# A decoder layer on one Trainium2 core: which PSUM bank side products may take in crowded slots, where dt's second part is placed, and a lock of its own for LayerNorm's tile

## The chip, the cores and the metric

The kernel runs on one NeuronCore of a Trainium2 chip. Its engines are TensorE (PE in the profile; PEld are its weight loads), VectorE (DVE), ScalarE (ACT), GpSimd (POOL) and SyncE (SP, which here only issues DMAs). Each engine works through its own instructions in the order in which the program lists them. The metric is the time of one execution on the device in microseconds; lower is better.

## What is computed

One pre-norm decoder layer on x of shape (16, 256, 512), in float32, with a context of the same shape:

```python
x = x + mamba2(layernorm(x))          # 32 heads of 64, state 64, convolution of 4 taps
x = x + xattn(layernorm(x), ctx, ctx) # sigmoid features, k times v summed over positions, then cumulative over heads
x = x + ffn(layernorm(x))             # ternary weights, 8 bit activations, gate and up 2048 wide
```

The attention part adds sigmoid(q wq + bq) times a state: sigmoid(k wk + bk) times the values, summed over the positions of a batch, and cumulative over the heads; the feed-forward part rounds its inputs to 8 bits and its weights to three values. The change lies in what surrounds the first part:

```python
def _mamba2(x, W_in, conv_w, conv_b, A_log, D_param, dt_bias, norm_w, W_out):
    xz = x @ W_in
    z, xBC, dt_proj = xz[..., :2048], xz[..., 2048:4224], xz[..., 4224:]
    xBC_c = silu(causal_conv_of_4_taps(xBC, conv_w) + conv_b)
    x_conv, B_ssm, C_ssm = xBC_c[..., :2048], xBC_c[..., 2048:2112], xBC_c[..., 2112:]
    dt = jax.nn.softplus(dt_proj + dt_bias)
    A = -jnp.exp(A_log)
    def step(h, inp_t):
        x_t, dt_t, B_t, C_t = inp_t
        dA = jnp.exp(A[None, :] * dt_t)
        h = dA[:, :, None, None] * h + dt_t[:, :, None, None] * x_t[..., None] * B_t[:, None, None, :]
        y_t = jnp.einsum('bhds,bs->bhd', h, C_t) + D_param[None, :, None] * x_t
        return (h, y_t)
    y = scan_over_positions(step) * silu(z)
    var = jnp.mean(jnp.square(y), axis=-1, keepdims=True)
    return (norm_w * (y * jax.lax.rsqrt(var + EPS))) @ W_out
```

## The kernel before

**Tiling.** The 16 batches are taken as 8 pairs k, the 2048 inner channels as 16 chunks c of 128. One step of the main loop is a slot s = 16 k + c: one chunk of one pair. The loop runs over s = 2 to 127, with its first two slots and a last part written out apart; then the feed-forward part goes over 32 tiles of 128 rows. In the profile the written-out start ends at about 45 us and the slots at about 1515 us.

**One slot's own work**, in TensorE's order: the projection to z (12 matmuls of 512 columns, L676), with turn_x (L941, four transposes of the last chunk's convolved x) put in after the sixth; the projection to x (12 more); scan_out of the last chunk (py, L961 and L968); the product with W_out for the chunk before that (po, L1011). VectorE: times_g, the product of the last chunk's decays with B and C's matrix (L929, L933); the chunk's two scans (L912); the three taps of the convolution (L693, writing xs); D x and the gate (L976, L981). ScalarE: silu of z (L891), the convolution's first tap (L897), silu of xs (L906), scalings (L920, L951) and others. GpSimd: the low halves of y (L988) and sums of squares (L999). So turn_x of a slot needs silu of the taps of the slot before, and scan_out needs times_g.

**The order is written by hand.** A slot has 8 points, now = 8 s + 0 to 7; at each, advance(now) lets side tasks (Python generators) issue their next step. A step says how many points to wait (wait), at which points of a slot it may be issued, on which engine and how many us it is taken to need; a planner's allowance (room, for VectorE 2.3 us in each half of a slot) holds it back when that engine has been given enough, unless the step is marked with leaves, which must go. Tasks are asked in the order of their rank. The side tasks are: LayerNorm of the next pair or of a batch's queries (norm_transposed), dt for the next pair (time_steps), B and C for the next pair (states), the context (context_pair, context_group), the rest of a batch's attention (batch_end) and the quantising of the feed-forward weights.

**dt** (time_steps) has these steps on VectorE: part 1 (L724 to L731), then exp on ScalarE (L733), part 2a (L735 to L739), part 2b (L742 to L745, a row of fourteen small operations with 2a), then exp, a transpose on TensorE and a short scan. **B and C** (states): a projection of 12 matmuls, the first tap on ScalarE (L791), three taps on VectorE (L693, writing bcT), then silu. **The residual** (mixed, four operations L1037 on VectorE, after L1028 and a power on GpSimd) is written out in the third slot of each pair from the third pair on (s = 34, 50, 66, ...), ahead of that slot's times_g.

**PSUM banks.** A side product needs a bank. Class Banks hands out two: "own", one tile kept for this, at point 7; and "z" at point 3, between the projection to x and scan_out, which is one tile of the ring ps_p with two buffers in which the slot's two projections stand:

```python
if self.free["z"] and others and others[0] is me:
    hold = "z"
```

With z taken, the next slot's first projection is the third tile after the x projection in a ring of two, so it waits until the taps have read that one.

**Locks.** Shared(n) is a counter of n that tasks take and give in the order of the program's making; it keeps a task from reusing a tile whose last user has not been issued. lns (1) guards LayerNorm's tiles: y ("ln", the normalised rows in float32), and its two float16 halves hi and lo, from which two transposing DMAs read. It was held from the load to the transposes. The small statistics tiles have two buffers.

**SP's queue** carries, in every slot, the loads of the decays (L837, L847) and of W_out's chunk (L538, two buffers: issued after L1011 of its slot, used two slots later), from some slots weights (L412), and the side tasks' transposes (L652), loads (L614, L1046, L1066, L1095) and stores (L1135, L1400).

Of the kernel before, what the change touches and what calls it, by code (L numbers as in the profile page):

```python
# [58 lines left out]
def decoder_kernel(  # L59
# [135 lines left out]
    with ExitStack() as part:  # L195
# [19 lines left out]
        WAIT = "wait"  # L215
# [3 lines left out]
        POINTS = 8  # L219
# [10 lines left out]
        def dve(us, wait=2):  # L230
            return (wait, (1, 2, 5, 6), "dve", us) if steady() else (soon(), range(POINTS), "dve", us)
# [30 lines left out]
        def leaves(step):  # L262

            return *step, True
# [3 lines left out]

        clock = [0]

        class Shared:
            def __init__(self, free):
                self.free = free
# [14 lines left out]
        class Banks:  # L288
# [8 lines left out]
            def take(self, own=False, first=False):  # L297
                me = [own]
                self.line.insert(0 if first else len(self.line), me)
                while True:  # L300
                    moment = clock[0] % POINTS
                    if steady() and moment == 3:

                        others = [one for one in self.line if not one[0]]
                        if self.free["z"] and others and others[0] is me:
                            hold = "z"
                            break
                    elif self.free["own"] and self.line[0] is me and (
                        not steady() or moment == 7 and clock[0] >= self.since
                    ):  # L310
                        hold = "own"
                        break
                    yield WAIT
                self.line = [one for one in self.line if one is not me]
                self.free[hold] = False
                return hold
# [8 lines left out]
        def misc(hold, shape, name):  # L325
# [2 lines left out]
            }[hold]  # L328
            return ps.tile(shape, F32, tag=tag, name=name)

        chunks, stages, lns, turned, turned_q, attends, ctxs, outs, xs, late, preps, streams = (
            Shared(n) for n in (3, 3, 1, 2, 1, 1, 1, 2, 3, 1, 2, 2)
        )


# [270 lines left out]
            yield  # L606
        def norm_transposed(src, b, what, store):

            yield from lns.take(rank=0 if what == "m" else 2 if "late" in store else 1)
            y = p1.tile([P, NT, D], F32, tag="ln", name=f"ln_{what}_{b}")  # L610
            if src is None:
                src = y
                yield moved(1.3, 1)
                nc.sync.dma_start(y, x[b].rearrange("(i p) d -> p i d", p=P))  # L614
                yield landed()
            mv = p2.tile([P, NT, 2], F32, tag="ln_mv", name=f"ln_mv_{what}_{b}")
            rs = p2.tile([P, NT], F32, tag="ln_rs", name=f"ln_rs_{what}_{b}")
            yield leaves(dve(1.7)) if what == "m" else dve(1.7)
            for i in range(NT):
                st = p2.tile([P, 6], F32, tag="ln_st", name=f"ln_st_{what}_{b}_{i}")  # L620
                nc.vector.bn_stats(st, src[:, i, :])
                nc.vector.bn_aggr(mv[:, i, :], st)
            nc.vector.tensor_scalar(rs, mv[:, :, 1], EPS, LN_UP**-2, ALU.add, ALU.mult)
            hi = p1.tile([P, NT, D], F16, tag="ln_hi", name=f"lnh_{what}_{b}")
            lo = p1.tile([P, NT, D], F16, tag="ln_lo", name=f"lnl_{what}_{b}")
            nc.vector.tensor_scalar(mv[:, :, 1], mv[:, :, 0], -1.0, None, ALU.mult)
            yield 1, range(POINTS), "pool", 1.5
            nc.gpsimd.tensor_tensor(rs, rs, mhalf[:, 0:NT], ALU.pow)
            nc.gpsimd.tensor_tensor(mv[:, :, 1], mv[:, :, 1], rs, ALU.mult)
            yield act(2.3, 2)  # L630
            for i in range(NT):
                nc.scalar.activation(
                    y[:, i, :], src[:, i, :], AF.Identity,
                    scale=rs[:, i : i + 1], bias=mv[:, i, 1:2],
                )
            nc.scalar.copy(hi, y)
            yield pool(2.4)
            nc.gpsimd.tensor_tensor(lo, y, hi, ALU.subtract)
            if what == "q":
                yield from turned_q.take(rank=2 if "late" in store else 1)  # L640
                store["q"] = [
                    p1.tile([P, NT, KD, P], F16, tag=f"lnT_{n}_q", name=f"lnT_{n}_q_{b}") for n in "hl"
                ]
                dst = store["q"]
            else:
                if b % 2 == 0:
                    yield from turned.take()
                    turned_tiles(store, b)
                dst = [t[:, b % 2] for t in store["lnT"]]
            for t, part_ in zip(dst, (hi, lo)):  # L650
                yield moved(1.2, 4 if part_ is hi else 1)
                nc.sync.dma_start_transpose(  # L652
                    t.rearrange("p i k t -> p (i k) t"), part_.rearrange("p i d -> p (i d)")
                )
            lns.give()
            if what == "q" or b % 2:
                yield landed(12 if what == "m" else 8)
                store["ready", what] = True
# [39 lines left out]
        def time_steps(pair):  # L698
# [3 lines left out]
            k = pair["k"]  # L702
            hold = yield from bank.take(first=True)
            pd = misc(hold, [P, NT, 2, NH], f"pd_{k}")
            for j in range(2):
                for i in range(NT):
                    n = 0
# [23 lines left out]
            nc.vector.scalar_tensor_tensor(v, r, -2.0, v, ALU.mult, ALU.add)  # L731
            yield alone()
            nc.scalar.activation(v, v, AF.Exp)  # L733
            yield dve(1.2)
            nc.vector.tensor_scalar(s, v, 2.0, None, ALU.add)  # L735
            nc.vector.reciprocal(s, s)
            nc.vector.tensor_tensor(s, s, v, ALU.mult)
# [39 lines left out]
        def states(pair):  # L777


            while ("ready", "m") not in pair:  # L780
                yield WAIT
            k = pair["k"]
            hold = yield from bank.take()
            raw = misc(hold, [P, 2, S], f"bc_{k}")
            project_pair(
                raw.rearrange("p b (i t) -> p (b i) t", i=NT), lambda wi, kc: w_bc16[:, wi, kc, :],
                pair,
            )
            yield leaves(act(0.8, 2))
            bcT = p1.tile([P, 2, S], F32, tag="bcT", name=f"bcT_{k}")  # L790
            nc.scalar.activation(  # L791
                bcT, raw, AF.Identity, scale=convw_bc[:, 3:4], bias=convb_bc
            )
            yield leaves(dve(2.3, 1))
            for j in (2, 1, 0):
                tap_of(bcT, raw, convw_bc, j)
            bank.give(hold)
            yield act(0.6)
            nc.scalar.activation(bcT, bcT, AF.Silu)
            yield issued()  # L800
            cT = p1.tile([NS, 2, S], F32, tag="cT", name=f"cT_{k}")
            if k:
                nc.sync.dma_start(cT, bcT[NS : 2 * NS])
            else:
                pc = misc("o3", [P, 2, S], "cT_first")
                nc.tensor.matmul(pc[0:NS], ident[:, NS : 2 * NS], bcT, start=True, stop=True)
                nc.scalar.copy(cT, pc[0:NS])
            yield landed()
            g = p2.tile([P, 2, 3, P], F32, tag="g", name=f"g_{k}")
            for j in range(2):  # L810
                yield pe(0.4)
                hold = yield from bank.take()
                pg = misc(hold, [P, 3, P], f"pg_{k}_{j}")
                for n, (s0, t0) in enumerate(((0, 0), (P, P), (0, P))):
                    nc.tensor.matmul(
                        pg[:, n, :], bcT[0:NS, j, s0 : s0 + P], cT[:, j, t0 : t0 + P],
                        start=True, stop=True,
                    )
                yield leaves(dve(0.7))
                nc.vector.tensor_tensor(  # L820
                    g[:, j, 0:2, :], pg[:, 0:2, :], upper.unsqueeze(1).to_broadcast([P, 2, P]),
                    ALU.mult,
                )
                nc.vector.tensor_copy(g[:, j, 2, :], pg[:, 2, :])
                bank.give(hold)
            pair["g"] = g
            yield
# [203 lines left out]
        def mixed(pair, ns=range(2 * NT)):  # L1031

            rq = pair["rq"]
            for n in ns:
                j, i = divmod(n, NT)
                xb = batches[2 * pair["k"] + j]["x"]
                nc.vector.scalar_tensor_tensor(  # L1037
                    xb[:, i, :], pair["po"][n], rq[:, n : n + 1], xb[:, i, :], ALU.mult, ALU.add
                )
# [463 lines left out]
        proj, m, tp, o2, o3 = (ps_p, "proj"), (ps_m, "m"), (ps_t, "tp"), (ps_o, "o2"), (ps_o, "o3")  # L1503
# [423 lines left out]
        for s in range(2, n_slots):  # L1927
# [5 lines left out]
            if u:  # L1933
                units[s + 2] = u
            if ended:
                mixed(ended)
                for j in range(2):
                    start(s, batch_end(batches[2 * ended["k"] + j]), rank=2)
# [147 lines left out]
```

## Time and profile before

| what | us |
|---|---|
| median of 3 runs (lowest, highest) | 1891.16 (1885.18, 1892.93) |
| the profiled execution's own time | 1887.74 |
| its span, first to last instruction | 1886.0 |
| PE busy in 0 to 45, 45 to 1515, 1515 to 1886 | 28.6, 1401.6, 351.7 |
| DVE busy in the same stretches | 33.1, 1275.7, 333.1 |
| ACT busy in the same stretches | 25.7, 969.0, 249.0 |
| POOL busy in the same stretches | 7.3, 625.2, 40.4 |

The mean granted clock of TensorE is 0.988 of full speed. The span is divided by the profile into 40 slices; in each, a digit is the busy share in tenths:

```profile
PE   6789999999999998999999999999999989999998
DVE  7899888777888889888988998989887879999997
```

TensorE is at nine tenths nearly everywhere, VectorE between seven and nine. A line of the table of groups has the line of the source, engine, operation, what is written and read, the count, and after the bar the busy time and the mean in ns:

```profile
L693 DVE SCALAR_TENSOR_TENSOR xs<-pp,convw_sb,xs 128x510 f32<-128x510 f32 (+2 forms) x384 | 286.3, 746 | 147.3 <-ACT xs L897 137.8
L912 DVE TENSOR_TENSOR_SCAN m<-dab,starts 128x512 f32<-128x512 f32 x254 | 302.4, 1232 | 0.0
```

The last part is the engine's idle time just before, with what ended most of it. A row of a table of waits is: engine and line that waited, "<-", what ended the wait, then us in total, how many times, and the longest. In a timeline the first column is the start in us, the second the duration, and a bracket at the end holds idle time before the instruction and what ended it.

### The profile page before, as it was taken

The numbers are of one execution on the slowest core, as the hardware profiler recorded it, in microseconds if no ns is written. First come the engines' busy times: TensorE is split into PE (matmuls) and PEld (weight loads), VectorE is DVE, ScalarE is ACT, GpSimd is POOL, SyncE is SP. The second block draws the span as 40 slices with busy tenths as digits, with TensorE's granted clock in tenths as the row PEclk, the third lists the DMA queues.
The fourth block names the chain that finished last, engine by engine and source line by source line (L and its number), as shares of the span: only waits on it lengthen the run. The fifth ranks groups of instructions, "written<-read, shape, count | busy, mean of one in ns | idle before, by whom it ended". The sixth has DMA issues, their size and how long they took to land.

```text
span 1886.0 us, 30370 instructions
## 1 busy us (share of the span) xinstructions
PE 1781.9 (94%) x10464; PEld 1016.7 (54%) x10464; DVE 1641.9 (87%) x2718; ACT 1243.6 (66%) x2889; POOL 673.0 (36%) x684
## 2 busy tenths in 40 slices
PE   6789999999999998999999999999999989999998
PEld 4355555555556555656555556555556544444443
DVE  7899888777888889888988998989887879999997
ACT  5677656676667665666666666666666647777675
POOL 1233433343334354546454536454532222100000
PEclk9899999999999999999999999999999999999999
DMA  5764775689669677877697779687777726555554
GB/s 168 235 185 147 234 197 176 210 261 233 171 180 296 185 196 232 264 177 183 209 251 211 202 198 266 192 190 184 246 198 200 250 70 123 133 115 122 107 118 98
DMA packets 296933, 358.95 MB, mean 190 GB/s; under 512 B 163765, under 2 KB 197861, under 8 KB 296778
## 3 DMA queue, kind: packets, MB, share of 16 engines
q1 hardware_dynamic: 277962, 296.13, 59.8%
q0 software_dynamic: 18240, 60.84, 9.4%
q8 instruction: 83, 1.36, 0.3%
q14 instruction: 72, 0.59, 0.1%
q10 hardware_dynamic: 576, 0.04, 0.0%
HBM read 279.70 MB, written 39.58 MB: 169 GB/s over the span
## 4 chain that ended last, share of the span: by engine, by line
PE 60%; DVE 25%; ACT 4%; DMA 4%; issue 4%; POOL 2%; SPq 0%; ACTq 0%; DVEq 0%; POOLq 0%
PE pp L676 22%; PE po L1011 12%; PE po_f L1621 5%; PE pu L1579 5%; PE pg L1579 5%; DVE m L912 4%; PE py L961 4%; DVE xs L693 4%; DVE m L929 2%; PE trx L941 2%; PE py L968 2%; DVE m L933 1%; DVE y L976 1%; DVE sp_q L742 1%; PE bc L676 1%
## 5 line engine op out<-in xcount | busy, mean ns | idle before, releaser
L676 PE MATMUL pp<-lnT_h_m,w 128*128 128x512 f16 (+1 forms) x2056 | 659.2, 382 | 21.9 <-DVE xs L693 21.1
L676 PEld LDWEIGHTS <-w 128*128 128x128 f16 x3084 | 295.9, 99 | 360.8 <-issue 34.3
L988 POOL TENSOR_TENSOR yl<-y,yh 128x512 fp32r<-128x512 f32 x128 | 179.9, 1406 | 712.5 <-ACT yh L987 627.2
L693 DVE SCALAR_TENSOR_TENSOR xs<-pp,convw_sb,xs 128x510 f32<-128x510 f32 (+2 forms) x384 | 286.3, 746 | 147.3 <-ACT xs L897 137.8
L676 PE MATMUL pp<-lnT_l_m,w 128*128 128x512 f16 (+1 forms) x1028 | 392.6, 382 | 0.0
L1011 PE MATMUL po<-wout,yh 128*128 128x512 f32 x1024 | 339.4, 413 | 6.7 <-DMA wout<-wout_d 5.5
L951 ACT ACTIVATE xdt<-trx,dt 128x64 f32<-128x64 f32 x1024 | 222.7, 328 | 161.6 <-PE trx L941 161.3
L912 DVE TENSOR_TENSOR_SCAN m<-dab,starts 128x512 f32<-128x512 f32 x254 | 302.4, 1232 | 0.0
L1011 PEld LDWEIGHTS po<-wout,yh 128*128 128x128 f32 x1024 | 185.3, 191 | 64.3 <-issue 16.7
L1011 PE MATMUL po<-wout,yl 128*128 128x512 f32 x512 | 205.0, 400 | 2.2 <-POOL yl L988 2.2
L906 ACT ACTIVATE xs<-xs 128x512 f32<-128x512 f32 x128 | 80.9, 632 | 190.7 <-DVE xs L693 190.7
L961 PE MATMUL py<-m,xdt 128*64 128x256 f32 x1024 | 162.5, 396 | 11.8 <-DVE m L933 5.9
L920 ACT ACTIVATE m<-edb,m 128x128 f32<-128x128 f32 x508 | 162.6, 395 | 12.6 <-DVE m L912 12.5
L1579 PEld LDWEIGHTS <-yT 128*128 128x128 bf16 x1024 | 99.7, 98 | 129.5 <-issue 12.1
L897 ACT ACTIVATE xs<-pp,convb_sb,convw_sb 128x512 f32<-128x512 f32 x128 | 100.2, 783 | 103.1 <-PE pp L676 103.1
L999 POOL TENSOR_TENSOR ssq<-ssq,sq 128x512 f32<-128x512 f32 x120 | 158.4, 1320 | 27.4 <-ACT sq L998 26.5
L929 DVE TENSOR_TENSOR m<-m,g 128x1024 f32<-128x1024 f32 x128 | 162.0, 1266 | 0.1
L1579 PE MATMUL pg<-w_ffn,yT 128*128 128x512 bf16 x512 | 131.4, 379 | 7.0 <-ACT h L1583 5.0
L1579 PE MATMUL pu<-w_ffn,yT 128*128 128x512 bf16 x512 | 131.4, 379 | 1.6 <-DVE h L1584 0.9
L1621 PE MATMUL po_f<-w_ffn,hT 128*128 128x512 bf16 x512 | 125.4, 379 | 1.9 <-DMA hT<-hq 1.8
L1583 ACT ACTIVATE h<-pg,sg 128x512 f32<-128x512 f32 x128 | 86.0, 681 | 48.0 <-PE pg L1579 47.7
L1011 PEld LDWEIGHTS po<-wout,yl 128*128 128x128 f32 x512 | 97.5, 190 | 28.5 <-POOL yl L988 5.0
(278 smaller groups left out, 2774.8 us busy)
## 6 DMA issues: line engine op xcount, KB each, us to landing
dab<-da_d SPq DMA_DIRECT2D x127, 512.0 KB
wout<-wout_d SPq DMA_DIRECT2D x112, 512.0 KB
edb<-ed_d SPq DMA_DIRECT2D x127, 256.0 KB
w<-w_d SPq DMA_DIRECT2D x40, 512.0 KB
raw<-in_w_zx SPq DMA_DIRECT2D x16, 512.0 KB
wout_d<-wout SPq DMA_DIRECT2D x16, 512.0 KB
ctxT<-in_ctx_t POOLq DMA_DIRECT2D x16, 512.0 KB, 8.4
x<-in_x SPq DMA_DIRECT2D x16, 512.0 KB
```

The costliest lines, as they stand in the source:

```text
L676: nc.tensor.matmul(dst, w(wi, kc), yT[yi][:, :, kc, :], start=n == 0, stop=n == 3 * KD - 1)
L693: nc.vector.scalar_tensor_tensor(u[:, :, d:S], raw[:, :, 0 : S - d], w[:, j : j + 1], u[:, :, d:S], ALU.mult, ALU.add,)
L912: nc.vector.tensor_tensor_scan(u["m"][:, 4 * j : 4 * j + 4, :].rearrange("p k t -> p (k t)"), u["da"][j].rearrange("p h i t -> p (h i t)") ...
L920: nc.scalar.activation(u["m"][:, 8 + n, :], u["ed"][:, n // 2, n % 2, :], AF.Copy, scale=u["m"][:, 2 * n, P - 1 : P],)
L929: nc.vector.tensor_tensor(m, m, gi.unsqueeze(2).to_broadcast([P, 2, 2, NT * P]), ALU.mult)
L951: nc.scalar.activation(u["xdt"][:, j, i, h, :], u["tr"][:, j, i, h * HD : (h + 1) * HD], AF.Copy, scale=dt[:, i, j, 2 * c + h : 2 * c + h ...
L961: nc.tensor.matmul(py[h * HD : (h + 1) * HD, j, :].rearrange("p (i t) -> p i t", i=NT), xdt[:, j, 0, h, :], m[:, 2 * (2 * j + h) : 9 + 2 * ...
L988: nc.gpsimd.tensor_tensor(lo, u["y"], hi, ALU.subtract)
L999: nc.gpsimd.tensor_tensor(pair["ssq"], pair["ssq"], sq, ALU.add)
L1011: nc.tensor.matmul(pair["po"][n], u["yhl"][yi][:, j, i * P : (i + 1) * P], w[:, wi, :], start=c == 0 and p == 0, stop=c == NU - 1 and p == 2,)
L1579: nc.tensor.matmul(dst, yT[:, kc, :], w_ffn[w + kc][:, cols], start=kc == 0, stop=kc == KD - 1)
L1621: nc.tensor.matmul(u["po"], u["hT", k // (KF // 2)][:, k % (KF // 2), :], w_ffn[2 * KD + k // NF][:, (k % NF) * D : (k % NF + 1) * D], sta ...
```

## The change

A mark, crowded[0], holds a moment on the planner's clock. It is set to 8 points ahead when B and C's taps are issued, and when a residual is. Until that moment is reached, no side product takes the z bank. dt's part 2a is asked to wait for the same moment, once, ahead of its step; that step's wait is 1 point in place of 2. LayerNorm's lock is split: lns now guards the tile y alone and is given as soon as GpSimd's subtract, the last reader of y, is issued; a new lock, halves, guards hi and lo from after the statistics to the transposes. The engines' instructions are the same, in other places.

```diff
@@ decoder_kernel
         clock = [0]
 
+        crowded = [0]
+
@@ Banks.take
                     if steady() and moment == 3:
 
                         others = [one for one in self.line if not one[0]]
-                        if self.free["z"] and others and others[0] is me:
+
+                        idle = clock[0] >= crowded[0]
+                        if self.free["z"] and idle and others and others[0] is me:
                             hold = "z"
                             break
@@
-        chunks, stages, lns, turned, turned_q, attends, ctxs, outs, xs, late, preps, streams = (
-            Shared(n) for n in (3, 3, 1, 2, 1, 1, 1, 2, 3, 1, 2, 2)
+        chunks, stages, lns, turned, turned_q, attends, ctxs, outs, xs, late, preps, streams, halves = (
+            Shared(n) for n in (3, 3, 1, 2, 1, 1, 1, 2, 3, 1, 2, 2, 1)
         )
@@ norm_transposed
-            yield from lns.take(rank=0 if what == "m" else 2 if "late" in store else 1)
+            rank = 0 if what == "m" else 2 if "late" in store else 1
+            yield from lns.take(rank=rank)
             y = p1.tile([P, NT, D], F32, tag="ln", name=f"ln_{what}_{b}")
...
             nc.vector.tensor_scalar(rs, mv[:, :, 1], EPS, LN_UP**-2, ALU.add, ALU.mult)
+            yield from halves.take(rank=rank)
             hi = p1.tile([P, NT, D], F16, tag="ln_hi", name=f"lnh_{what}_{b}")
             lo = p1.tile([P, NT, D], F16, tag="ln_lo", name=f"lnl_{what}_{b}")
...
             nc.gpsimd.tensor_tensor(lo, y, hi, ALU.subtract)
+            lns.give()
...
                 nc.sync.dma_start_transpose(
                     t.rearrange("p i k t -> p (i k) t"), part_.rearrange("p i d -> p (i d)")
                 )
-            lns.give()
+            halves.give()
@@ time_steps
             nc.scalar.activation(v, v, AF.Exp)
-            yield dve(1.2)
+            while k and clock[0] < crowded[0]:
+                yield WAIT
+            yield dve(1.2, 1)
             nc.vector.tensor_scalar(s, v, 2.0, None, ALU.add)
@@ states
             yield leaves(dve(2.3, 1))
+            crowded[0] = clock[0] + POINTS
             for j in (2, 1, 0):
                 tap_of(bcT, raw, convw_bc, j)
@@ main loop
             if ended:
+                crowded[0] = now + POINTS
                 mixed(ended)
```

## The prediction

> **What bounds the kernel now.** I read the page first: its span, and the chain that ended last.
>
> ```profile
> span 1886.0 us, 30370 instructions
> ...
> PE 60%; DVE 25%; ACT 4%; DMA 4%; issue 4%; POOL 2%; SPq 0%; ACTq 0%; DVEq 0%; POOLq 0%
> ```
>
> TensorE (PE) is the bound, and VectorE (DVE) takes its place for a quarter of the chain. To see where, I asked for TensorE's waits in the part of the loop whose order the change can touch (436 to 1400 us).
>
> ```profile
> PE pp L676 <- DVE xs L693: 21.1, 12, 3.5
> PE py L961 <- DVE m L933: 4.6, 5, 1.1
> PE trx L941 <- ACT xs L906: 3.1, 4, 1.3
> PE pk L1246 <- DVE kp L1231: 2.4, 1, 2.4
> PE po L1011 <- DMA wout<-wout_d: 1.9, 1, 1.9
> ```
>
> With three smaller rows (0.7, 0.5, 0.2) TensorE waits 34.5 us there. The first row is the change's target: the first product of the next slot waits for the convolution taps L693, because a side product holds the other buffer of the "proj" ring. Next, the timeline of TensorE and the table by stretch at the worst case (slot 104).
>
> ```profile
> 1270.68 0.39 PE L1122 MATMUL pa<-z,q 96*128 96x512 f32 x1
> 1274.55 0.61 PE L676 MATMUL pp<-lnT_h_m,w 128*128 128x512 f16 x1 [3.48 <-DVE xs L693]
> 1274.95 0.63 PE L676 MATMUL pp<-lnT_l_m,w 128*128 128x512 f16 x1
> ```
>
> ```profile
> 1266.00:1274.50 8.50, 5.07 (x30) 3.44 (x30) 8.29 (x11) 2.83 (x7) 3.85 (x2) 0.95 0.80 185
> 1274.50:1281.00 6.50, 6.45 (x19) 2.92 (x20) 6.40 (x9) 4.58 (x13) 0.00 (x0) 0.54 0.50 169
> ```
>
> Columns: length, busy time of PE, PEld, DVE, ACT, POOL, granted clock, DMA share, GB/s. VectorE is busy 8.29 of 8.50 us: it is not waiting for anyone. After the stall the granted clock is 0.54, and matmuls start 0.43 us apart, against 0.216 otherwise. The same table gives 0.54, 0.54 and 0.55 in 3.4 us from 529, 901 and 1123 us and 0.52 in 6.8 us from 1273 us: 17 us at half clock, 8.5 us lost. Stalls and half clock together are 43 us, the most that any reordering can win. What VectorE did meanwhile:
>
> ```profile
> 1263.44 0.74 DVE L693 SCALAR_TENSOR_TENSOR bcT<-bc,convw_bc,bcT 128x506 f32<-128x506 f32 x1
> ...
> 1265.83 3.37 DVE L912 TENSOR_TENSOR_SCAN m<-dab,starts 128x512 f32<-128x512 f32 x2
> 1269.13 1.25 DVE L735 TENSOR_SCALAR sp_s<-sp_v 128x128 f32<-128x128 f32 x1
> ...
> 1272.19 2.30 DVE L693 SCALAR_TENSOR_TENSOR xs<-pp,convw_sb,xs 128x510 f32<-128x510 f32 x3
> ...
> 1278.13 2.33 DVE L912 TENSOR_TENSOR_SCAN m<-dab,starts 128x512 f32<-128x512 f32 x2
> 1280.38 1.90 DVE L742 SCALAR_TENSOR_TENSOR sp_q<-sp_q,sp_s 128x128 f32<-128x128 f32 x6
> ```
>
> The B/C taps, dt's part 2a (L735 to L739: 1269.13 to 1272.19, 3.06 us) and 2b (L742 to L745: 1280.38 to 1284.12, 3.74 us; four other pairs took 4.56, 6.01, 4.73 and 4.71, mean 4.75) stand ahead of the taps. So in these slots the reader sees two queues, and VectorE's is the longer.
>
> **Prices.** VectorE's own work in a slot, start to start in a quiet one: products L929/L933 1.73, scans 2.25, taps 2.23, y 1.38: 7.6 us against TensorE's 10.08 (24 projection matmuls of 0.216, turn_x 0.44, L961/L968 1.5, L1011 2.9). So 2.5 us a slot are free for side work.
>
> **Part A, side products leave z's bank.** In the order as built, the flag refuses the bank in slots 34, 39, 50, 55, 72, 82, 88, 105 and 114. Only four of the twelve stalls lie there: 34 (1.96), 39 (0.61), 72 (3.09), 88 (0.31), 6.0 us. In slots 40, 56, 73, 83, 89, 91 and 104 another side product still holds it (slot 99's 0.32 us goes, as none happens to be due): the flag lasts 8 points from the taps and is over when 2b comes, a slot later. And a freed bank does not free TensorE: after six matmuls (1.30 us) turn_x L941 needs the silu L906 (0.63) of the same taps. With the bank held, turn_x began 0.57 us after that silu in slots 34 and 39 (0.85 in 72); that is all that is won. Slot 72 gains nothing: VectorE works almost without a break from 888 to 917 us, so what TensorE saves it waits for one slot later. Sum: 0.57 + 0.57 + 0.31 = -1.4 us (from -6.0 if turn_x never binds, to 0). The products themselves (0.2 to 1.2 us each) are moved to the own bank or a later slot, not removed.
>
> **Part B, dt's second part.** The task is past its wait at point 5, before the taps set the flag at point 6, in pairs 3 to 7; in pairs 1 and 2 it waits, but is issued where it was. In pairs 3, 5 and 6 its place is unchanged. In pairs 4 and 7 the shorter wait (1 point for 2) puts 2a into the same half slot as the B/C taps, 3 points earlier. Working for slot 54 (pair 4; 104 is alike), time 0 at its L961: taps end at 2.9 (convolution on ScalarE ends 0.89 after the last projection matmul, a 0.22 us side product lies between, then 2.23). ScalarE then does silu 0.63, a table load 1.28 and exp 0.31, so 2a runs 5.1 to 8.2, the B/C taps (2.24) to 10.4, products (1.73) to 12.2. TensorE wants them at 10.08: it waits 2.1. Queued behind are its next L961, L1011 and two slots of products. From there the next taps' silu ends after scans 2.25 + 2b 4.75 + taps 2.23 + silu 0.73 = 9.96 us; TensorE reaches turn_x after 1.5 + 2.9 + 1.30 and pk's 1.0 (pair 4) or pa's 0.23 (pair 7), 6.7 or 5.9: it waits 3.3 and 4.0. Stalls: 2 x 2.1 + 3.3 + 4.0 = 11.5. Waits of 3.09 and 3.26 us were followed by 3.4 us at half clock and 3.48 by 6.8; so add 1.7 and 3.4: 16.6. Gone are pair 4's waits of 2.71, 2.40, 0.60 and 0.71 and pair 7's 3.48 with its 3.4 of half clock: 13.3. Net +3.3. Ends: 2b at 3.74 and no half clock gives 4.2 + 2.3 + 3.0 = 9.5, so -3.8; 2a stretched by 1.5 (L738 took 0.29 but once 1.81) and 2b at 6.0 give 3.6 x 2 + 4.6 + 5.3 = 17.1, with half clock after all four (1.7 + 1.7 + 3.4 + 3.4) 27.3, so +14. I take the mean rows.
>
> For the clock the Trainium skill has a rule ("TensorE: Matmul & The Clock Gate", section "Part 1: The HAM clock gate (the "warmup" mystery)"): about 3.4 us of idling halve it. The trace is stricter, 3.09 us sufficed, and 1.86 us did after eight matmuls of 16 columns at 1123 us. By the rule only the 4.0 us wait would count, and the net of B would be 11.5 + 3.4 - 13.3 = +1.6. It speaks against a change that gathers waits into one.
>
> **Part C, the LayerNorm tile's own lock.** Statistics blocks (2 x 0.70 + 2 x 0.16 + 0.32 + 0.12 = 2.2 us on VectorE) start up to two slots earlier. Batch 9's falls into slot 50, right behind the residual (L1037, 2.73 us): taps end at 641.9 + 2.2 = 644.1, silu at 644.8, TensorE could turn at 637.58 + 1.5 + 2.9 + 0.23 + 1.30 = 643.5: +1.3 (0 to +2). Around pair 6 the block of batch 9's queries goes from slot 90 to 87, and slot 91 keeps 0.7 of about 3 us ahead of its taps: its 1.86 us wait and 1.7 of half clock go, while 2.2 + 0.3 - 0.6 us more work, less some 0.3 us of idle VectorE, is met in slots 87 to 89: -2 (-4 to +1). The other blocks fall into free VectorE time, 2.5 us a slot; uncovered, each costs up to 2.2.
>
> Its DMAs: each LayerNorm has one load and two transposes (2.6 to 4.0 us each on SP). The loads for batches 8, 9, 10, 12 and 14 pass ahead of one wout and of decay loads; a load now also waits on SP for GpSimd's subtract L638 (2.15 us), with those behind it. Cover: a wout is issued after L1011 of its slot and needed two slots, 20 us, later. I take 0; gone cover costs about the one 1.9 us wait, which followed eight z_d stores that held SP from 945.97 to 954.43. Those of group 3 now come a slot later, nearer to two transposes. GpSimd's steps are as many as before, and L988 idles 712 us in all. In the last phase only batch 15's statistics move: 0, behind TensorE's own work.
>
> **Sum.** -1.4 + 3.3 + 1.3 - 2 = +1.2 us. The profiled execution took 1887.74 us (span 1886.0 and 1.74 around it), 3.4 below the median of the runs: 1888.9 on its scale, 1892.4 on the median's.
>
> **Rivals.** (1) The bank is the bound. All twelve waits and the half clock gone: 1891.2 - 21.1 - 8.5 = 1861.6. For it: the largest row. Against: seven of the places stay, and the silu stands 0.6 us behind. What is possible of it: the four flagged waits 6.0, half clock at 901 (1.7), slot 91's 3.6, dt at no cost: -11.3, 1880. Chance 0.13.
> (2) Slower by one mechanism: 2a and the B/C taps in one half slot make the products L929/L933 late, in slots 54 and 104. It decides once that wait passes 3 us, where half clock follows every stall: B at +14, C at +2: 1907. For it: VectorE stretches (L912 2.2 for 1.2 us). Chance 0.25.
> (3) The change doesn't do what it says for dt and moves VectorE's queue without shortening it: the forecast, chance 0.62.
>
> **How the numbers follow.** 0.5% is 9.5 us, about what a measurement of this kernel can tell from no change. The forecast's own range is B from its low end to half way to its high one with the rest as taken, -5.9 to +6.6: 1885 to 1898. The range reaches toward both rivals: 1883 to 1905. Faster 0.13, same 0.62, slower 0.25.
>
> **What would show it.** TensorE's "pp from xs" row falls from 21.1 to some 8 to 14 us; in its place "trx from ACT xs" rises from 3.1 to about 8 or more, and "py from DVE m" from 4.6 to 8 or more, with waits of 2 to 3 us just ahead of slots 55 and 105. Part A is wrong if turn_x does not wait where the bank is free; B if 2a is not next to the B/C taps in pairs 4 and 7. A fall of TensorE's idle time by 10 us or more, or half clock gone altogether, would make the forecast wrong.

## The result, and the profile after

The changed kernel takes 1902.44 us in the median of 6 runs (1900.24 to 1908.49) against 1890.82 us for the kernel before (6 runs). The ratio is 1.0068, with a 95% interval of 1.0052 to 1.0084: it is slower, by a little over the 0.5% that can be told from no change. The profiled execution took 1908.49 us.

From the page of the changed kernel, its span and the chain that ended last. Lines of the source lie 7 to 10 further down than before (L676 is now L683, L961 is L971, L1037 is L1047):

```profile
span 1906.8 us, 30374 instructions
...
PE 62%; DVE 20%; DMA 7%; ACT 6%; issue 3%; POOL 1%; SPq 0%; ACTq 0%; POOLq 0%; DVEq 0%
```

VectorE's share of the chain fell from 25% to 20%, as was meant, but DMA's rose from 4% to 7%. TensorE's waits in the changed part of the loop, 436 to 1420 us (in total, how often, the longest):

```profile
PE py L971 <- DVE m L943: 13.7, 5, 6.3
PE trx L951 <- ACT xs L916: 10.6, 8, 3.3
PE pp L683 <- DVE xs L700: 4.4, 3, 2.5
...
PE pq L1033 <- DVE y L986: 2.1, 1, 2.1
```

The row that the change aimed at fell from 21.1 to 4.4 us. Two others took it over: turn_x, which needs silu of the same taps, rose from 3.1 to 10.6, and scan_out, which needs times_g, from 4.6 to 13.7. One entry of that row, 6.3 us, is longer than any wait in this part of the kernel before (3.5). Its cause is among VectorE's own waits, from 400 to 1540 us:

```profile
DVE x L1047 <- POOL rq L1039: 9.3, 6, 2.9
DVE x L1047 <- DMA x<-in_x: 9.0, 1, 9.0
```

In the kernel before, no residual waited for the rows it is added to. Here one did, for 9.0 us. The timelines of SP, VectorE and TensorE about it, in that order:

```profile
1197.68 0.61 SPq L1145 DMA_DIRECT2D x_d<-x  x1
1198.39 4.58 SPq L1105 DMA_DIRECT2D z<-z_d  x3
1210.67 0.38 SPq L1056 DMA_DIRECT2D x<-in_x  x1
```

```profile
1195.87 0.66 DVE L1136 TENSOR_TENSOR x<-x,pa 128x512 f32<-128x512 f32 x1
...
1204.16 1.41 DVE L1047 SCALAR_TENSOR_TENSOR x<-po,rq,x 128x512 f32<-128x512 f32 x2 [1.17 <-POOL rq L1039]
1214.59 1.41 DVE L1047 SCALAR_TENSOR_TENSOR x<-po,rq,x 128x512 f32<-128x512 f32 x2 [9.02 <-DMA x<-in_x]
```

```profile
1217.88 1.12 PE L971 MATMUL py<-m,xdt 128*64 128x256 f32 x4 [6.32 <-DVE m L943]
```

This is pair 5's residual, written out in slot 98. Its batch 10 is done at 1205.57; batch 11's rows have not come. They need a buffer of which there are three, and the one that falls to them is batch 8's, which is free only when the attention of batch 8 has added its last product (1195.87, L1136) and the store of x (1197.68) has landed. The load then goes out at 1210.67, 13.0 us after that store was issued, and its reader goes on 3.9 us later. In the kernel before, the load went out some 20 us ahead of the residual:

```profile
1166.97 1.55 SPq L1135 DMA_DIRECT2D x_d<-x  x1
1168.61 2.22 SPq L1095 DMA_DIRECT2D z<-z_d  x3
1174.46 0.37 SPq L1046 DMA_DIRECT2D x<-in_x  x1
```

In the order as built, batch 8's last two products moved from slots 93 and 94 to slot 96, and with them the load of batch 11's rows from slot 95 to slot 97. That is called "late rows" below. The table by stretch (length, busy time of PE, PEld, DVE, ACT, POOL, then granted clock, DMA share, GB/s) shows what comes on top:

```profile
1204.10:1207.50 3.40, 3.40 (x15) 1.82 (x12) 1.41 (x2) 0.14 (x2) 0.63 (x2) 0.54 1.04 386
1207.50:1214.30 6.80, 4.06 (x18) 1.62 (x16) 0.00 (x0) 4.06 (x12) 3.92 (x3) 0.98 0.77 248
1214.30:1221.10 6.80, 3.22 (x17) 2.30 (x18) 6.44 (x10) 1.39 (x4) 3.49 (x5) 0.53 0.72 270
```

VectorE has 0.00 us of work in the middle stretch, and in the first and the last TensorE ran at about half clock.

**Where the time went.** From the first scan_out product of slot 34 to that of slot 127, TensorE's time can be taken apart into its waits, half of the time at half clock, and the rest:

| profiled execution | loop, us | waits | lost at half clock | rest |
|---|---|---|---|---|
| before | 1065.8 | 34.3 | 8.5 | 1023.0 |
| after | 1079.5 | 41.2 | 15.4 | 1023.0 |

The rest is the same to the tenth, but by some luck: half clock while TensorE waits is counted in both terms, 0.4 us before and 2.4 after. Counted once, it leaves a rest of 1023.4 and 1025.4, so all but 2 of the 13.7 us are waits and clock. By slots (how much later a slot's scan_out begins than in the kernel before, taken as differences), 11.0 us of the 13.7 lie in slot 97, which now ends with the 6.32 us wait (10.9 in the second profile, after_again); all else sums to 2.7. The other 7 us of the two spans lie ahead of slot 34, where both programs have the same order, and behind slot 127.

### The profile page after: what moved, and what is told of

The parts are those of the page before. It is cut to its first block, busy times and chain, and to the rows that moved or that the text cites. A ratio compares the mean times of both kernels' runs of the same rounds, so it can differ in the third digit from the quotient of the medians.

```text
span 1906.8 us, 30374 instructions
## 1 busy us (share of the span) xinstructions
PE 1794.2 (94%) x10464; PEld 1022.1 (54%) x10464; DVE 1629.5 (85%) x2718; ACT 1244.6 (65%) x2889; POOL 674.5 (35%) x684
## 4 chain that ended last, share of the span: by engine, by line
PE 62%; DVE 20%; DMA 7%; ACT 6%; issue 3%; POOL 1%; SPq 0%; ACTq 0%; POOLq 0%; DVEq 0%
PE pp L683 23%; PE po L1021 12%; PE po_f L1631 5%; PE pu L1589 5%; PE pg L1589 5%; PE py L971 4%; DVE xs L700 4%; DVE m L922 3%; PE trx L951 2%; PE py L978 2%; DVE m L939 2%; ACT xdt L961 1%; PE bc L683 1%; DVE m L943 1%; DVE y L991 1%
## 5 line engine op out<-in xcount | busy, mean ns | idle before, releaser
L683 PE MATMUL pp<-lnT_h_m,w 128*128 128x512 f16 (+1 forms) x2056 | 659.0, 382 | 5.9 <-DVE xs L700 4.8
L683 PEld LDWEIGHTS <-w 128*128 128x128 f16 x3084 | 295.8, 99 | 344.7 <-issue 35.6
L683 PE MATMUL pp<-lnT_l_m,w 128*128 128x512 f16 (+1 forms) x1028 | 392.3, 382 | 0.0
L961 ACT ACTIVATE xdt<-trx,dt 128x64 f32<-128x64 f32 x1024 | 222.7, 328 | 182.9 <-PE trx L951 182.4
L971 PE MATMUL py<-m,xdt 128*64 128x256 f32 x1024 | 164.3, 399 | 25.9 <-DVE m L943 15.4
L939 DVE TENSOR_TENSOR m<-m,g 128x1024 f32<-128x1024 f32 x128 | 158.0, 1235 | 0.1
```

Of the source, the lines that this page charges most:

```text
L683: nc.tensor.matmul(dst, w(wi, kc), yT[yi][:, :, kc, :], start=n == 0, stop=n == 3 * KD - 1)
L939: nc.vector.tensor_tensor(m, m, gi.unsqueeze(2).to_broadcast([P, 2, 2, NT * P]), ALU.mult)
L961: nc.scalar.activation(u["xdt"][:, j, i, h, :], u["tr"][:, j, i, h * HD : (h + 1) * HD], AF.Copy, scale=dt[:, i, j, 2 * c + h : 2 * c + h ...
L971: nc.tensor.matmul(py[h * HD : (h + 1) * HD, j, :].rearrange("p (i t) -> p i t", i=NT), xdt[:, j, 0, h, :], m[:, 2 * (2 * j + h) : 9 + 2 * ...
```

## The experiments

Kernels of one group ran beside the same runs of the kernel before. "Ratio" is to these, with its 95% interval; "waits" and "half" are the two terms of the table above, in the profiled execution, where the kernel before has 34.3 and 8.5.

| kernel | median, us | before, us | ratio (interval) | waits | half |
|---|---|---|---|---|---|
| after_z80 | 1897.38 | 1889.84 | 1.0042 (1.0029, 1.0055) | 34.7 | 8.5 |
| bank_80 | 1909.88 | 1889.84 | 1.0106 (1.0090, 1.0121) | 51.2 | 15.4 |
| x11_late | 1893.84 | 1889.84 | 1.0014 (1.0001, 1.0028) | 35.5 | 13.7 |
| x11_mid | 1889.94 | 1889.84 | 0.9997 (0.9986, 1.0008) | 30.4 | 8.5 |
| after_again | 1901.99 | 1888.22 | 1.0072 (1.0051, 1.0093) | 41.8 | 15.4 |
| dt_only | 1895.08 | 1888.22 | 1.0033 (1.0018, 1.0047) | 38.5 | 11.9 |
| lock_only | 1899.19 | 1888.22 | 1.0047 (1.0030, 1.0065) | 37.1 | 11.9 |
| bank_60 | 1901.82 | 1888.22 | 1.0063 (1.0042, 1.0084) | 40.6 | 11.9 |
| no34 | 1888.43 | 1890.62 | 0.9994 (0.9978, 1.0010) | 30.2 | 10.2 |
| no60 | 1895.78 | 1890.62 | 1.0026 (1.0013, 1.0039) | 34.4 | 8.5 |
| split3 | 1895.62 | 1890.62 | 1.0028 (1.0012, 1.0044) | 32.9 | 9.5 |
| c457 | 1886.33 | 1888.59 | 0.9992 (0.9978, 1.0006) | 27.3 | 8.5 |

In all of them the loop less these two terms is 1017 to 1025 us, and with half clock during waits counted once 1023 to 1026.

How far a single profile can be trusted is shown by x11_mid. TensorE, VectorE and ScalarE have the order of the kernel before there, to the last instruction, and its loop is still 3.6 us shorter. Slot 91 alone, ahead of the load that is held, is 3.7 us shorter: a wait of 1.86 us and the half clock behind it are missing. So a step of 2 to 4 us in one slot of one profile can be chance.

**1. The changed kernel without the refusals of slots 82 and 88** (after_z80).

```diff
-                        idle = clock[0] >= crowded[0]
+                        idle = clock[0] >= crowded[0] or 80 <= clock[0] // POINTS < 96
```

> The changed kernel, but z's bank is not refused in slots 80 to 95 (the refusals of slots 82 and 88 go, those of 34 to 72, 105 and 114 stay; dt's wait and the lock stay). Theory 'late rows': the two refusals push batch 8's attention two slots back, its x buffer comes free two slots later, and the rows of batch 11 land 9 us after pair 5's residual wants them. Without them the load goes out two slots earlier, VectorE never waits for x<-in_x, and the time falls by 10 to 12 us, from 1902 to 1890 to 1893. Rival 'collision': dt's second part beside the convolution of B and C costs the time; it stands in slots 54 and 102 as before, so the time stays at 1899 to 1904.

In its trace VectorE never waits for x<-in_x, and the load stands at 1169.62, behind a store at 1163.05. The waits and the half clock are back at the old sums, and slot 97 is no longer than before. The profiled loop is 2.8 us above the kernel before, 10.9 below the changed kernel: the wait was due to these two refusals. The median moved less: 0.42% above before in place of 0.68% and 0.72%, about 5 us, with intervals that just overlap, and lies between the two ranges expected. So late rows are part of the loss, and some 8 us are something else. (In its own order the refusal of slot 105 is gone too; the last ones fall into slots 98, 103 and 114.)

**2. These refusals alone** (bank_80: the kernel before, with the flag heeded in slots 80 to 95 only).

```diff
-                        if self.free["z"] and others and others[0] is me:
+                        idle = clock[0] >= crowded[0] or not 80 <= clock[0] // POINTS < 96
+                        if self.free["z"] and idle and others and others[0] is me:
```

> The kernel before with the refusal of z's bank in slots 80 to 95 alone; dt's wait and the LayerNorm lock as before. Late rows: the load of batch 11's rows goes out in slot 97 as in the changed kernel, VectorE waits 7 to 10 us for it, and the time rises by 8 to 13 us to 1899 to 1904. Rival 'collision': two refusals and no dt step moved, 1889 to 1893.

Late rows hold, at a larger price than expected: the residual waits 17 us.

```profile
DVE x L1041 <- DMA x<-in_x: 17.0, 1, 17.0
```

```profile
PE pp L679 <- DVE xs L696: 20.2, 9, 3.7
PE py L965 <- DVE m L937: 18.7, 5, 13.9
```

Here the store went out at 1192.60, the load 14.8 us after it and 5.5 us more until the residual could go on. TensorE's wait is 13.9 us, with 17.07 us at half clock from 1204.2 us. This kernel lost 1.06%, more than the whole change: the changed kernel has the same late load, and its residual comes later.

**3. The load alone, held back** (x11_late, x11_mid: the kernel before, with 97 and 96).

```diff
             yield from xs.take()
+            while b == 11 and clock[0] < 97 * POINTS + 5:
+                yield WAIT
             yield moved(1.3, 1)
```

> The kernel before, of which nothing is changed but that the load of batch 11's rows is held until slot 97, where the changed kernel issues it (before: slot 95). Late rows: the same wait of 7 to 10 us on VectorE in slot 97 or 98, and 8 to 14 us in all, 1899 to 1905. Rival: a load off the chain is hidden, 1889 to 1893.

> As the run that holds the load of batch 11's rows, but only until slot 96, one slot later than in the kernel before. Late rows: the rows land some 10 us earlier than from slot 97, that is 1 to 2 us before the residual wants them at best or 1 to 3 us after it at worst, so at most 3 us are lost: 1890 to 1894. If each slot of delay costs alike, half of what the hold to slot 97 costs.

Held to slot 96 it costs nothing, held to slot 97 only 0.14%, with a wait of 1.35 us:

```profile
1189.14 1.25 SPq L652 DMA_TRANSPOSE lnT_h_m<-lnh_m  x1
1190.45 0.58 SPq L1048 DMA_DIRECT2D x<-in_x  x1
```

```profile
1196.92 1.41 DVE L1037 SCALAR_TENSOR_TENSOR x<-po,rq,x 128x512 f32<-128x512 f32 x2 [1.35 <-DMA x<-in_x]
```

The expectation took the load's place in the program for its time. Here batch 8's store is long over, so the load goes out at 1190.45, 3 us after slot 97 begins; in the changed kernel, placed in the same slot, it stands behind its buffer's store and goes out 16 us after the slot begins. What costs is the buffer that comes free late, not the load that is asked for late.

**4. The change again, and its parts alone.** dt_only has the flag and dt's wait, lock_only the split lock, bank_60 the refusals ahead of slot 60, each added to the kernel before. In bank_60's own order these are in slots 34, 39, 50 and 56, not 55.

```diff
+            while k and clock[0] < crowded[0]:
+                yield WAIT
-            yield dve(1.2)
+            yield dve(1.2, 1)
...
+                        idle = clock[0] >= crowded[0] or clock[0] // POINTS >= 60
```

> The changed kernel unaltered, a second profile and its time beside the single parts. Late rows: VectorE waits again 8 to 10 us for x<-in_x in slot 97, and the time is 1900 to 1904. If that wait was a chance of the one profiled execution, it is absent here, at a time of still 1900 to 1904.

> The kernel before with dt's changed wait alone (its flag set, but z's bank never refused, and one LayerNorm lock). dt's second part stands beside the convolution of B and C in slots 55, 86 and 103, once more than in the changed kernel; batch 11's load goes out in slot 94, so nothing of the late rows is in it. Late rows, with the prediction's collision at +1 a piece: 1890 to 1894. If the collision is what is left in the run without the refusals of slots 82 and 88 (7 us): 1896 to 1900.

> The kernel before with the LayerNorm tile's own lock alone. Batch 9's load goes out three slots earlier, in slot 76, batch 11's as before, so no late rows. The prediction has -1 to +1 for the lock: 1888 to 1892. If the lock is what is left of the loss: 1896 to 1900.

> The kernel before with the refusal of z's bank in slots 34, 39, 50 and 55 alone. Batch 11's load goes out in slot 95 as before, so no late rows. The prediction has -1 for the refusals: 1888 to 1891. If a refusal costs by itself, by moving products into TensorE's own bank, 2 us each: 1896 to 1900.

The wait recurs in the second profile of the changed kernel (8.9 us on VectorE, 6.3 on TensorE), so it is no chance of one execution. Each part alone makes the kernel slower, by 0.33%, 0.47% and 0.63%, with no late rows in any. dt_only lies between its two ranges, lock_only in the second, bank_60 above both. Together the three would be 1.4%, twice what the change costs, though they hold only four of its nine refusals: they don't add. All of the first part's nine refusals without the rest were not run: in the order that they make, pair 6's residual comes up before batch 13 has a buffer for its rows.

The surprise is where the time is lost. Taken from slot 34 on, bank_60 is 2.4 us ahead of the kernel before at slot 58, with its four refusals behind it; at slot 127 it is 11.0 behind. lock_only is 2.5 behind at slot 58 and 5.7 at the end, dt_only 1.7 ahead and 6.8 behind. Of bank_60, the rows of TensorE's waits that the kernel before lacks or has smaller:

```profile
PE trx L945 <- ACT xs L910: 6.0, 5, 3.0
PE q L1080 <- DMA lnT_l_q<-lnl_q: 3.1, 1, 3.1
...
PE po L1015 <- POOL yl L992: 2.4, 2, 2.0
PE zp L1382 <- ACT zs L895: 1.9, 1, 1.9
PE q L1080 <- ACT zs L895: 1.7, 1, 1.7
```

The q products wait for a LayerNorm's transposes (slot 78), po for GpSimd (68), zp for ScalarE's silu of z (99): none stands beside a refusal. (The longest of turn_x, 3.0 us, does: it is in slot 56.) lock_only has the same wait of q in slot 79, 2.7 us.

**5. Is it the place that costs, or the new order?** no34 refuses the bank in one crowded slot: by its trace, eight small products of TensorE and one copy of VectorE come half a slot later. no60 refuses it in one slot that is not crowded at all: four groups of the context's products come half a slot later in slots 60 to 63, and one step of quantising the feed-forward weights is made up for only in slots 110 to 112.

```diff
-                        if self.free["z"] and others and others[0] is me:
+                        if self.free["z"] and clock[0] // POINTS != 60 and others and others[0] is me:
```

> The kernel before with z's bank refused in slot 34 alone, a slot with a residual on VectorE; it moves a few products within slots 34 to 40 and nothing after. Theory 're-deal': what a moved product costs is not paid where it stands but by the new order that the planner makes of everything after it; here hardly anything follows, so within 2 us of before: 1887 to 1891. Rival 'place': the refusal itself costs, by putting products into TensorE's own bank, 2 to 4 us: 1891 to 1894.

> The kernel before with z's bank refused in slot 60 alone, a slot with neither a residual nor the convolution of B and C, in which one product of the context's moves by half a slot; the planner's order differs from there to the end of the loop, and all loads of rows stay in their slots. Re-deal: a neutral place costs like any other whose order spreads, 4 to 10 us: 1893 to 1900. Place: nothing is gained or lost where VectorE has room: 1887 to 1892.

The refusal in the crowded slot is free (0.9994), the one in the quiet slot costs 0.26%. Both lie in the ranges of 're-deal' and outside those of 'place'. In the profiled execution of no60 the largest loss against the kernel before is 2.7 us in slot 65, five slots after the refusal, where a residual follows. VectorE there, in no60 and then in the kernel before:

```profile
822.04 2.73 DVE L1037 SCALAR_TENSOR_TENSOR x<-po,rq,x 128x512 f32<-128x512 f32 x4 [2.66 <-POOL rq L1029]
824.69 1.22 DVE L929 TENSOR_TENSOR m<-m,g 128x1024 f32<-128x1024 f32 x1
825.82 1.75 DVE L933 TENSOR_TENSOR m<-m,g 128x512 f32<-128x512 f32 x1
827.50 2.33 DVE L912 TENSOR_TENSOR_SCAN m<-dab,starts 128x512 f32<-128x512 f32 x2
```

```profile
817.80 2.73 DVE L1037 SCALAR_TENSOR_TENSOR x<-po,rq,x 128x512 f32<-128x512 f32 x4 [1.76 <-POOL rq L1029]
820.44 1.22 DVE L929 TENSOR_TENSOR m<-m,g 128x1024 f32<-128x1024 f32 x1
821.57 0.69 DVE L933 TENSOR_TENSOR m<-m,g 128x512 f32<-128x512 f32 x1
822.17 3.42 DVE L912 TENSOR_TENSOR_SCAN m<-dab,starts 128x512 f32<-128x512 f32 x2
```

GpSimd's power comes 0.9 us later after L1028, L933 takes 1.06 us longer, and scan_out waits 1.82 us where it had none. The kernel before has a stretch of the same size one instruction later (L912, 3.42 against 2.33), where TensorE does not wait for it. So in this profile part of the price was paid away from the refused slot; four others that keep the old order there (x11_late, x11_mid, bank_80, no34) have no such step. Where the rest of the 5 us lies isn't shown: this execution's loop is only 1.3 us longer, and its time is 6.4 below the median of the kernel's other runs.

That the price goes with the spread of the new order is not shown either, and no60 speaks against it. From one scan_out to the next, TensorE's instructions stand in another order than in the kernel before in only 5 places, VectorE's in 6; in c457 below it is 20 and 28, and c457 isn't slower. Over all runs there is a pattern, but no rule: every kernel whose VectorE has another order in 42 places or more is slower by 0.28% or more; of those with fewer, c457 (28), no34 (2) and x11_mid (0) are not slower, x11_late (16) is by 0.14% and no60 (6) by 0.26%.

**6. Smaller pieces of dt.** split3 cuts dt's polynomial into four pieces in pairs 2 to 7; c457 only in pairs 4, 5 and 7, where the order of everything else changes little outside slots 56 to 62, 72 to 78 and 104 to 115.

```diff
             nc.vector.reciprocal(s, s)
+            if k in (5,):
+                yield dve(1.2)
...
             for n in (13, 11, 9, 7, 5, 3):
+                if n == 5 and k in (4, 5, 7):
+                    yield dve(1.7)
```

For split3 both conditions on k are k > 1.

> The kernel before with dt's polynomial on VectorE cut from two pieces (3.1 and 4.8 us) into four in pairs 2 to 7, each with its own place in the planner's order; batch 11's rows are asked for in slot 95 as before, batch 15's two slots later. If the waits of TensorE for xs that stand beside dt's pieces (slots 40, 56, 57, 72, 104: 2.4 to 3.5 us each in the kernel before) come of their size, they halve and with the half clock that they bring the time falls by 6 to 12 us: 1878 to 1884. Re-deal: the new order costs 4 to 10 us and takes the gain back: 1886 to 1894.

> The kernel before with dt's polynomial cut once more in pair 4, twice more in pair 5 and once more in pair 7, chosen because the order of all other work then stays nearly as it was (all rows are asked for in the slots of before; outside slots 56 to 62, 72 to 78 and 104 to 112 nearly nothing moves). Re-deal: without a new order downstream the gain at the cut pieces is kept: of the waits in slots 56, 57, 72, 73 and 104 (13.6 us in the kernel before) a third to a half goes, with the half clock that stands beside two of them: 4 to 9 us less, 1882 to 1887. Rival: the pieces only hand the wait to the next slot, 1888 to 1892.

split3 does in its place what was expected: from slot 36 to slot 73 it gains 8.9 us. Then it loses 6.2 in slot 79 and 4.6 in slot 82, with the longest wait for the taps of its loop there (3.87 us in slot 79), and ends 0.28% slower. c457 has the fewest waits of all (27.3 us) and a profiled loop 7.3 us below the kernel before, 3.7 of them in slot 91 as in x11_mid, but its median is only 2.3 us lower and the interval of its ratio holds 1: not told apart from the kernel before. No version here is shown to beat the kernel before.

## Why the prediction was right or wrong

The forecast was 1892.4 us, no change that can be told; measured are 1902.4. The range, 1883 to 1905, holds it, but only because it was drawn out toward rival (2), slower with a chance of 0.25; the forecast's own range, 1885 to 1898, does not, and the 0.68% lie above the 0.5% that it counted as the same. As the cause that the runs show, the late rows, stands nowhere in the prediction, that the range holds is luck.

**Right: the waits change names.** The forecast had the row for the taps at 8 to 14; it fell further, to 4.4. It had turn_x at 8 or more (10.6) and scan_out at 8 or more (13.7, but 7.4 without the late rows). turn_x does wait where the bank is free, 3.30 us in slot 72 where the taps' wait was 3.09, as part A said. The waits ahead of slots 55 and 105 were to be 2.1 us; they are 2.54 and 2.55. The first, in the timeline of TensorE in the changed kernel:

```profile
705.10 0.65 PE L971 MATMUL py<-m,xdt 128*64 128x256 f32 x4 [2.54 <-DVE m L943]
```

**Wrong: "I take 0" for the DMAs.** This is the step that failed. It went through the loads and transposes of LayerNorm and through W_out on SP's queue. The rows of x, whose load waits for a buffer that the attention of an earlier batch holds, were in the list of SP's loads but not in the sum. Measured in the profiled execution: 11.0 of the loop's 13.7 us. Without them the loop is 2.7 us longer, against the forecast's 1.2; that the two are close is chance, as the terms below are further off and cancel.

**Wrong: "-1.4" for part A**, or rather the assumption under it, that a product moved to another bank or slot costs nothing more. Slots 34 to 45 come out 0.5 us longer; and two of the refusals, priced at 0 and -0.31, are those behind the late rows. bank_60 shows the same for refusals without late rows: 2.4 us won up to slot 58, 13.4 lost behind it.

**Part B was mis-sized, with its sign.** Pair 4's stretch (slots 53 to 58) is 3.5 us shorter, pair 7's (102 to 107) 1.5: -5.1 in place of +3.3, below its low end of -3.8; after_again has -2.8 and -1.0. Not all of it is dt's: the stretches hold refusals too, and bank_80, where dt is not touched, has -2.2 in slots 102 to 107. The first waits came near what was worked out (2.5 for 2.1 us), with 3.41 us of half clock behind each that was not forecast; the second, of turn_x, measured 0.53 and 1.74 us where 3.3 and 4.0 were forecast, and the half clock forecast behind these did not come. In after_again it is the other way round: no half clock behind the first waits, but second waits of 2.08 and 3.31 us, each with 3.41 us of half clock. dt_only's +0.33% is not in these slots: it is ahead at slot 58.

**Part C came close in one place:** slot 50 has +1.8 (+1.3 forecast), and so it has in after_again and after_z80. Slots 87 to 91 have -2.5 (-2), but x11_mid has -2.3 there in the order of the kernel before, so this is no evidence for the lock. Not seen were slots 80 to 82, together +3.6 (2.1 in after_again) and under no heading; bank_80 has 1.8 of it in slot 82, where the bank is refused. lock_only's +0.47% again lies elsewhere.

**Rival (2)** ended on the right side by the wrong mechanism: the collision in slots 54 and 104 was to cost 14 us. It is there and costs less than what it replaced.

**The clock.** The Trainium skill ("TensorE: Matmul & The Clock Gate", section "Part 1: The HAM clock gate (the "warmup" mystery)") has some 3.4 us of idling as the limit. The runs here are against it for a single wait: after 2.54 us ahead of slot 55 the clock is halved for 3.41 us from 706.1 us. But 2.5 us is no limit either: in after_again the same wait (2.56 us) is not followed by half clock. In the loops of the fourteen profiles, half clock begins during or within 1.1 us after 36 of 37 waits of 2.9 us or more, and 10 of 15 of 2.5 to 2.8 us.

**What stays open.** The changed kernel without late rows is still 0.42% slower in the median, but its profiled loop has the waits and the half clock of the kernel before. The profiled executions don't stand in one relation to the others: with late rows they are 5.0, 6.2 and 10.1 us above the median of the kernel's other runs (bank_80, after, after_again); of the rest, the kernel before's first one and nine of the others are 1.9 to 8.2 us below, dt_only's 2.1 above. So the 11 us are a profiled price. By the medians of after_z80 and the changed kernel, late rows cost about 5 us, and about 8 come with the rest of the change; no profile here shows where they lie, and no run why nearly every new order is slower than the one before.

## What to carry to other kernels

In an order that a planner makes, a moved step is not priced by the slot it leaves: follow each tile and lock that it or its successors hold to the next user, down to the load that waits for the buffer, and ask how far ahead of its reader that load goes out (some 20 us in the kernel before; after, its reader waited 9 us). Compare the issue place of every load in both orders, not only of those that the diff names. And take single parts alone on the chip: here the lock, dt's wait and four of the nine refusals cost 0.3 to 0.6% each, and the whole change 0.7%, so a sum of local prices, of either sign, is a weak forecast here.

## What the runs showed of the hardware

From the issue of a store to that of the load that reuses its buffer (512 KB each) it took very different times: 6.6 us in after_z80, 7.5 in the kernel before, 13.0 in the changed kernel and 14.8 in bank_80. In all four the three loads of z stand between the two on SP's queue; they held it for 2.2, 2.2, 4.6 and 5.5 us. The share of the DMA engines was 1.04 in the stretch from 1194 to 1204 us in the changed kernel.

The same wait can bring half clock in one execution and not in the next: the one in slot 56, of 2.67 to 2.71 us, is followed by 3.41 us of it in x11_late, x11_mid, no34, no60 and c457, and not in the kernel before and bank_80. In the changed kernel the clock was also halved at 1204.4 us, where TensorE had only waited 2.09 us and had then run 48 small products (1 or 128 columns), and in bank_80 it stayed so for 17.07 us, where all other stretches in the loops were 3.41, 6.83 or 10.24 us long.
